# Selective scan: the B product, the carry copy and the C product of two state groups as one instruction of twice the width

## The chip, the core and the metric

The kernel runs on one core of a Trainium2 chip. The metric is the device time of one execution in microseconds (us); lower is better. The engines named below are TensorE (PE in the profile, its weight loads PEld), VectorE (DVE), ScalarE (ACT), GpSimd (POOL) and SyncE (SP), which issues every DMA of this kernel.

## What is computed

The input is a batch of eight images of 96 channels on 64 x 64 pixels, all in float32. Layer 0 is a state-space block: group norm, layer norm, an input projection, a depthwise 3x3 convolution with SiLU, a selective scan in four directions, an output norm with a gate, an output projection, and a small convolution branch. Layer 1 is a linear attention without softmax and a feed-forward network in a low-precision format. What fills the time is the scan of layer 0:

```python
def step(h, inp):
    u_t, d_t, b_t, c_t = inp
    dA = jnp.exp(d_t[..., None] * A)
    h = dA * h + (d_t * u_t)[..., None] * b_t[:, :, None, :]
    y = jnp.einsum('bkdn,bkn->bkd', h, c_t)
    return (h, y)
```

It runs over 4,096 steps, for 8 images, 4 directions, 192 channels and 16 states each.

## The kernel before

The images are taken in four pairs. For a pair `p`, a direction `k` (0 to 3) and a piece `ci` of 1,024 of the 4,096 steps there are three jobs, one for each tile `T` of 128 rows: channels 0 to 127 of the first image, the same of the second, and the remaining 64 channels of both. Within a job, a group `j` (0 to 3) is 32 of those 128 channels. A group is four units, `q` = 0 to 3: one unit holds 32 channels x 4 states on 128 partitions and 1,024 time steps along the free axis. There are 192 jobs, 768 groups and 3,072 units. The main loop goes over the units two at a time, which gives 1,536 passes, here called pairs of units.

One unit is worked like this:

- `spread` (once for each group, TensorE): matmuls with a selection matrix copy the group's rows of `du` (delta times u) four times onto 128 partitions of the PSUM tile `pu` of 1,024 columns. There is one such tile.
- `weights` (SyncE): DMAs bring the unit's rows of B and C, broadcast to the 32 channels, as the SBUF tiles `bm` and `cm`. They stay for several groups and are loaded again when the image or the piece changes.
- `decay` (ScalarE): `da` is exp(delta * A), one instruction for each unit, at most four units ahead.
- `scan` (VectorE): the B product `pb = pu * bm` into PSUM (two tiles, one for each unit of the pair), then the recurrence itself, `hc = scan(da, pb)`, from PSUM and SBUF into SBUF. In the first piece of a direction the scan begins at zero, in the other three at the stored `carry`.
- `scan` (GpSimd): where a further piece follows, the last column of `hc` is copied to `carry`; then the C product `hc = hc * cm` in place.
- `total` (once for each group, TensorE): matmuls with `add` sum the four states on neighbouring partitions and the four units into the PSUM tile `yp`. ScalarE copies that to `y` and SyncE stores it. It is recorded one group late.

The order of all instructions on TensorE, VectorE, ScalarE and GpSimd is the order in which the Python code records them (`InOrder`, whose line 266 is therefore the line of nearly all of them in the profile). For one pair it is: background work by `slots.run()`, `scan` for both units, the loads of B for two pairs ahead and of C for one pair ahead, the two `decay`s of the next pair, and at `q` = 2 also `spread` of the next group and `total` of the one before; then `slots.run()` again. `slots.run()` records a little of the other work of the block (norms, convolutions, projections, gates, the step sizes of the next job) on TensorE, ScalarE, GpSimd and SyncE, under a budget for each slot; VectorE has next to nothing else while the scans go on.

In `scan`, the order on VectorE for one pair is: product of the first unit, product of the second, scan of the first, scan of the second. On GpSimd it is: carry, C product, carry, C product. `bm` has four buffers, `cm` five, `hc` eight, `da` four, each of 1,024 columns. Four of PSUM's eight banks hold the two `pb` tiles, two hold `pu`, and `yp` and `pg` have one each. The framework adds the semaphore waits: an instruction that reads or overwrites what another one wrote or reads waits for a count of the other's engine, and it does so too where both are on the same engine.

Of the kernel before, what the change touches and what calls it, by code (L numbers as in the profile page):

```python
# [9 lines left out]
F32 = mybir.dt.float32  # L10
# [4 lines left out]
ALU = mybir.AluOpType  # L15
# [12 lines left out]
CH = 1024  # L28
NCH = L // CH
# [321 lines left out]
def phase_b(  # L351
# [7 lines left out]
    nc = tc.nc  # L359
    with ExitStack() as ctx:  # L360
# [57 lines left out]
        for i in range(2):  # L418

            t = cp.tile([C + 1, 512], F32, name=f"tn{i}")  # L420
            nc.gpsimd.memset(t[C : C + 1, :], 1.0)
            tns.append(t)
        inner = ExitStack()
        bcp = inner.enter_context(tc.tile_pool(name="b_bc", bufs=4))
        wp = inner.enter_context(tc.tile_pool(name="b_w", bufs=2))
        hp = inner.enter_context(tc.tile_pool(name="b_h", bufs=8))
        gp = inner.enter_context(tc.tile_pool(name="b_bg", bufs=1))
        psc = inner.enter_context(tc.tile_pool(name="b_ps", bufs=1, space=PSUM))

# [4 lines left out]
        yps = psc.tile([128, 512], F32, name="yp")  # L434
        bank0 = psc.tile([128, 512], F32, name="pg")
        pu = psc.tile([128, CH], F32, name="pu")
        pbs = [psc.tile([128, CH], F32, name=f"pb{i}") for i in range(2)]
        pe = InOrder(tc, nc.tensor, mybir.EngineType.PE)
        ve = InOrder(tc, nc.vector, mybir.EngineType.DVE)
        se = InOrder(tc, nc.scalar, mybir.EngineType.Activation)  # L440
        ge = InOrder(tc, nc.gpsimd, mybir.EngineType.Pool)
# [5 lines left out]
            for ci in range(NCH) for T in (0, 2, 1)  # L447
        ]
        units = [(job, j, q) for job in range(len(jobs)) for j in range(4) for q in range(4)]
        carries, bcs, dus, dls, sts, das, hcs, prevs, yet = ({} for _ in range(9))  # L450
        turned, resting, squeezed_at = set(), set(), set()

        def where(job):
            p, k, ci, T = jobs[job]
            c = NCH - 1 - ci if k >= 2 else ci
            return p, k, ci, c, T, slice(c * CH, c * CH + CH)

        def batch(u):
            job, j, q = units[u]
            T = jobs[job][3]  # L460
            return j // 2 if T == 2 else T
# [806 lines left out]
        def weights(u, i):  # L1268

            if u >= len(units):  # L1270
                return
            job, j, q = units[u]
            p, k, ci, c, T, at = where(job)
            b = batch(u)
            if (job // 3, b, q, i) in bcs:
                return
            t = bcp.tile([128, CH], F32, name=("bm", "cm")[i], bufs=(4, 5)[i])
            r0 = 32 * (k // 2) + 16 * i + 4 * q
            nc.sync.dma_start(
                t, xd_d[k % 2][2 * p + b][r0 : r0 + 4, at].unsqueeze(0).to_broadcast([32, 4, CH])  # L1280
            )
            bcs[job // 3, b, q, i] = t

# [27 lines left out]
        def scan(u):  # L1311

            job, j, q = units[u]
            p, k, ci, c, T, at = where(job)
            step, last = (-1, 0) if k >= 2 else (1, CH - 1)
            for i in range(2):
                ve.tensor_mul(pbs[i], pu, bcs[job // 3, batch(u), q + i, 0])
            for i in range(2):
                t = hp.tile([128, CH], F32, name="hc")
                carry = carries[p, k][:, T, 4 * j + q + i : 4 * j + q + i + 1]  # L1320
                ve.tensor_tensor_scan(
                    t[:, ::step], das.pop(u + i)[:, ::step], (pbs[i])[:, ::step],
                    0.0 if ci == 0 else carry, ALU.mult, ALU.add,
                )
                hcs[u + i] = t
            for i in range(2):
                v = u + i
                carry = carries[p, k][:, T, 4 * j + q + i : 4 * j + q + i + 1]
                if ci < NCH - 1:
                    ge.tensor_copy(carry, hcs[v][:, last : last + 1])  # L1330
                ge.tensor_mul(hcs[v], hcs[v], bcs[job // 3, batch(u), q + i, 1])

        def before(g):

# [14 lines left out]
        def total(g):  # L1349


            job, j, _ = units[4 * g]
            p, k, ci, c, T, at = where(job)
            yp = yps[:, 0:256]
            if k >= 2:
                pe.matmul(yp, ident, prevs.pop(g), start=True, stop=False)
            if k == 2 and p > 0:
                pe.matmul(yp, ident, yet.pop(g), start=False, stop=False)
            for n in range(4):
                for i in range(4):  # L1360
                    pe.matmul(
                        yp[32 * i : 32 * i + 32, :], add,
                        hcs[4 * g + n][:, 256 * i : 256 * i + 256],
                        start=(n == 0 and k < 2), stop=(n == 3),
                    )
            for n in range(4):
                hcs.pop(4 * g + n)
            y = wp.tile([128, 256], F32, name="y")
            to = y_d if k == 2 else ys_d[1]

            def store():
                if k < 2:
                    nc.sync.dma_start(ya_d[k % 2][p][T][c, j], y)
                    return
                for i in range(4):
                    nc.sync.dma_start(
                        to[p][T][
                            32 * j : 32 * j + 32, c * CH + 256 * i : c * CH + 256 * i + 256
                        ],
                        y[32 * i : 32 * i + 32, :],  # L1380
                    )

            slots.after(1, lambda: se.copy(y, yp))
            slots.after(4, store)
# [4 lines left out]
        n = len(units)  # L1389
# [3 lines left out]
        for u in range(4):  # L1393
            weights(u, 0)
        for u in range(2):
            weights(u, 1)
# [3 lines left out]
        for u in range(0, n, 2):  # L1400
            g, q = divmod(u, 4)
            if q == 0:
                if g % 4 == 0:
                    job = g // 4 + 1
                    assert slots.first is None
                    p, k, ci, T = jobs[g // 4]
# [15 lines left out]
                    if job < len(jobs):  # L1422
                        p, k, ci, c, T, at = where(job)
# [4 lines left out]
            elif g + 2 < n // 4:  # L1428
                fetch(g + 2)
            slots.run()  # L1430
            scan(u)
            for v in range(u + 4, u + 6):
                weights(v, 0)
# [4 lines left out]
            if q == 2:  # L1438
                if g + 1 < n // 4:
                    spread(g + 1)  # L1440
                if g > 0:
                    total(g - 1)
# [3 lines left out]
        slots.run()  # L1446
        slots.run()
        total(n // 4 - 1)
        while not slots.idle():
            slots.run()  # L1450
# [18 lines left out]
        p = NP - 1  # L1469
# [336 lines left out]
def block(tc, a, out):  # L1806
    with tc.tile_pool(name="dram", bufs=1, space=DRAM) as dp:
# [29 lines left out]
        with tc.tile_pool(name="p_const", bufs=1) as pp:  # L1837
            phase_b(
                tc, a, pp, xi_d, xd_d, dl_d, ya_d, ys_d, y_d, zs_d, inp_d, x1_d, ua_d, u_d, g_d,
                cb_d, tn_d, out,  # L1840
            )
# [105 lines left out]
```

## Time and profile before

| | us |
|---|---|
| median of 3 runs | 11066.46 |
| the runs | 11069.53, 11062.12, 11066.46 |
| span of the profiled execution, first to last instruction | 11058.4 |
| VectorE busy in it | 10525.7 (95%) |
| GpSimd busy in it | 9028.7 (82%) |
| TensorE busy in it | 7887.2 (71%) |
| ScalarE busy in it | 6596.3 (60%) |
| VectorE: 3,072 B products, 128x1024 | 3601.6 (mean of one 1.220) |
| VectorE: 2,304 scans with a carry | 5276.8 (mean 2.334) |
| VectorE: 768 scans from zero | 1713.1 (mean 2.275) |
| GpSimd: 3,072 C products, 128x1024 | 7230.0 (mean 2.359) |
| GpSimd: 2,304 carry copies, 128x1 | 422.5 (mean 0.183) |

Of the profiled execution no time beside its span is listed. The median lies 8.1 us above the span, which is taken as what lies around it. The busy time of a row is the union of its instructions, so where instructions of one row overlap it is less than count times mean. The B products run from 214.6 us to 10719 us; ahead of them lie the norms and convolutions of the first pair of images, behind them the tail for the last pair.

### The profile page before, as it was taken

What the parts mean: (1) busy time and instruction counts of PE and PEld (TensorE: products, weight loads), DVE (VectorE), ACT (ScalarE), POOL (GpSimd) and SP (SyncE); (2) the same over time, 40 slices, a digit from 0 to 9 for tenths busy, and PEclk for the clock granted to TensorE, in tenths of its full rate; (3) what the DMA queues carried; (4) which work ended last, traced back from release to release, by engine and by line L of the source; (5) the groups of instructions that cost most, each with busy time, mean ns of one, the idle gap of its engine ahead of it and who ended that gap; (6) DMA issues with size and microseconds to landing.
All of it is one profiled execution on the core that took longest, in us unless ns stands there. A gap on an engine that the chain in (4) does not pass through costs nothing.

```text
span 11058.4 us, 128094 instructions
## 1 busy us (share of the span) xinstructions
PE 7887.2 (71%) x39468; PEld 3111.6 (28%) x39468; DVE 10525.7 (95%) x6651; ACT 6596.3 (60%) x9175; POOL 9028.7 (82%) x6649
## 2 busy tenths in 40 slices
PE   7755778655568887767777787776767776665778
PEld 3322333222223332223222332223322222222223
DVE  4999999999999999999999999999999999999974
ACT  2544765544567666556776656565776656665554
POOL 2788877787898888998888887899889888988860
PEclk8877888877788888878878888887878877777889
DMA  3445554454555555666545555566544555644551
GB/s 117 151 165 180 160 156 157 141 188 156 163 185 172 171 172 157 211 214 195 158 152 160 157 178 159 177 220 209 172 157 159 160 164 179 197 157 140 173 157 37
DMA packets 900188, 1834.20 MB, mean 166 GB/s; under 512 B 247965, under 2 KB 421214, under 8 KB 892462
## 3 DMA queue, kind: packets, MB, share of 16 engines
q1 hardware_dynamic: 899502, 1826.01, 52.8%
q8 instruction: 314, 5.14, 0.2%
q14 instruction: 372, 3.05, 0.1%
HBM read 1405.13 MB, written 420.42 MB: 165 GB/s over the span
## 4 chain that ended last, share of the span: by engine, by line
PE 32%; issue 29%; DVE 17%; POOL 11%; ACT 6%; DMA 4%; SPq 0%; DVEq 0%; POOLq 0%; ACTq 0%
PE pu L266 12%; PE yp L266 11%; DVE hc L266 11%; POOL hc L266 7%; PE pg L266 6%; DVE pb L266 5%; ACT u L266 2%; ACT da L266 2%; POOL u L266 2%; PE t L266 2%; PE ps L197 1%; DMA bm<-xd 1%; POOL turn L266 1%; POOL carry L266 1%; ACT L266 1%
## 5 line engine op out<-in xcount | busy, mean ns | idle before, releaser
L266 POOL TENSOR_TENSOR hc<-hc,cm 128x1024 f32<-128x1024 f32 x3072 | 7230.0, 2359 | 591.0 <-DVE hc L266 382.6
L266 DVE TENSOR_TENSOR_SCAN hc<-da,carry,pb 128x1024 f32<-128x1024 f32 x2304 | 5276.8, 2334 | 38.1 <-ACT da L266 31.5
L266 PE MATMUL pu<-du,c_sel 128*128 128x512 f32 x3072 | 2452.5, 944 | 2244.1 <-DVE pb L266 2239.6
L266 DVE TENSOR_TENSOR pb<-pu,bm 128x1024 f32<-128x1024 f32 x3072 | 3601.6, 1220 | 133.9 <-PE pu L266 105.9
L266 ACT ACTIVATE da<-dl,c_alog 128x1024 f32<-128x1024 f32 x3072 | 3352.8, 1140 | 91.4 <-DVE hc L266 73.8
L266 PEld LDWEIGHTS pu<-du,c_sel 128*128 128x128 f32 x3072 | 790.0, 281 | 3521.1 <-DVE pb L266 2784.8
L266 DVE TENSOR_TENSOR_SCAN hc<-da,pb 128x1024 f32<-128x1024 f32 x768 | 1713.1, 2275 | 38.9 <-ACT da L266 22.8
L266 ACT COPY y<-yp 128x256 f32<-128x256 f32 x768 | 284.4, 370 | 2348.9 <-PE yp L266 2198.4
L266 PE MATMUL yp<-hc,c_add 128*32 128x256 f32 x24576 | 1660.8, 416 | 22.6 <-ACT s L266 6.6
L266 PEld LDWEIGHTS yp<-hc,c_add 128*32 128x32 f32 x24576 | 768.6, 120 | 1200.1 <-issue 628.4
L266 POOL COPY carry<-hc 128x1 f32<-128x1 f32 x2304 | 422.5, 183 | 766.1 <-DVE hc L266 744.9
L266 ACT ACT_TABLE_LOAD x566 | 726.2, 1283 | 38.2 <-DMA cb<-zs 16.9
L266 ACT COPY u<-pg 128x512 f32<-128x512 f32 (+6 forms) x397 | 218.3, 550 | 712.3 <-PE pg L266 641.2
L266 POOL TENSOR_TENSOR u<-u,u 96x512 f32<-96x512 f32 (+1 forms) x426 | 537.5, 1269 | 105.9 <-ACT u L266 101.8
L266 POOL TENSOR_TENSOR du<-du,dls 128x1024 f32<-128x1024 f32 x192 | 452.7, 2358 | 91.5 <-ACT dls L266 91.1
L266 ACT COPY u<-yp 96x512 f32<-96x512 f32 (+6 forms) x347 | 188.0, 542 | 465.5 <-PE yp L266 404.5
L266 PE MATMUL pg<-ain,wmain 96*128 96x512 f32 x792 | 354.1, 599 | 0.0
L266 PE MATMUL pg<-ain,wmix 96*128 96x512 f32 x792 | 353.0, 598 | 0.0
L266 PE MATMUL yp<-prev,ident 128*128 128x256 f32 x768 | 321.9, 512 | 39.0 <-ACT u L266 27.4
L266 PEld LDWEIGHTS yp<-prev,ident 128*128 128x128 f32 x768 | 214.5, 283 | 381.8 <-issue 264.3
L266 PE MATMUL pg<-st,dtw 12*128 12x512 f32 x384 | 218.5, 649 | 49.4 <-ACT u L266 28.8
L266 PE MATMUL yp<-st,dtw 12*128 12x512 f32 x384 | 227.9, 674 | 18.3 <-ACT u L266 10.9
(340 smaller groups left out, 7030.2 us busy)
## 6 DMA issues: line engine op xcount, KB each, us to landing
dl<-dl SPq DMA_DIRECT2D x768, 512.0 KB
bm<-xd SPq DMA_DIRECT2D x512, 512.0 KB
cm<-xd SPq DMA_DIRECT2D x512, 512.0 KB
du<-xi SPq DMA_DIRECT2D x192, 512.0 KB
dl<-dls SPq DMA_DIRECT2D x192, 512.0 KB
ya<-y SPq DMA_DIRECT2D x384, 128.0 KB
prev<-ya SPq DMA_DIRECT2D x384, 128.0 KB
xi<-u SPq DMA_DIRECT2D x152, 256.0 KB
```

The costliest lines, as they stand in the source:

```text
L197: nc.tensor.matmul(bank[r, :].rearrange("p (h w) -> p h w", w=W), w[:, t if len(which) > 1 or w is wmix else 0, columns], pads[b][:, 8 * j ...
L266: op(*args, **kw)
```

## The change

The two units of a pair share tiles of twice the width. `pb` becomes one PSUM tile of 2 x 1,024 columns in the same four banks, `hc` one SBUF tile of 2 x 1,024 with four buffers in place of eight, `bm` and `cm` tiles of 2 x 1,024 with two and three buffers, each still filled by two DMAs of the same size as before. The B product of a pair is then one VectorE instruction of 2,048 columns, in which `pu` is read twice by a step of zero. The carry copy is one GpSimd instruction of two columns, and the C product one GpSimd instruction of 2,048. The scans stay single. `total` reads the halves of the wide tiles with the same matmuls. The extra buffer space for `cm` (4 KB on each partition) comes from a smaller scratch area for DMAs that GpSimd would issue; here it issues none.

The order on VectorE for a pair becomes: product of both, scan of the first, scan of the second. On GpSimd: carry of both, C product of both.

```diff
-        hp = inner.enter_context(tc.tile_pool(name="b_h", bufs=8))
+        hp = inner.enter_context(tc.tile_pool(name="b_h", bufs=4))
...
-        pbs = [psc.tile([128, CH], F32, name=f"pb{i}") for i in range(2)]
+        pb = psc.tile([128, 2, CH], F32, name="pb")
...
-            t = bcp.tile([128, CH], F32, name=("bm", "cm")[i], bufs=(4, 5)[i])
+            if q % 2 == 0:
+                pairs[job // 3, b, q, i] = bcp.tile(
+                    [128, 2, CH], F32, name=("bm", "cm")[i], bufs=(2, 3)[i]
+                )
+            t = pairs[job // 3, b, q - q % 2, i]
             r0 = 32 * (k // 2) + 16 * i + 4 * q
             nc.sync.dma_start(
-                t, xd_d[k % 2][2 * p + b][r0 : r0 + 4, at].unsqueeze(0).to_broadcast([32, 4, CH])
+                t[:, q % 2, :], xd_d[k % 2][2 * p + b][r0 : r0 + 4, at].unsqueeze(0).to_broadcast([32, 4, CH])
             )
...
+            ve.tensor_mul(
+                pb, pu.unsqueeze(1).to_broadcast([128, 2, CH]), bcs[job // 3, batch(u), q, 0]
+            )
+            t = hcs[u] = hp.tile([128, 2, CH], F32, name="hc")
+            at = 4 * j + q
+            carry = carries[p, k][:, T, at : at + 2]
             for i in range(2):
-                ve.tensor_mul(pbs[i], pu, bcs[job // 3, batch(u), q + i, 0])
-            for i in range(2):
-                t = hp.tile([128, CH], F32, name="hc")
-                carry = carries[p, k][:, T, 4 * j + q + i : 4 * j + q + i + 1]
                 ve.tensor_tensor_scan(
-                    t[:, ::step], das.pop(u + i)[:, ::step], (pbs[i])[:, ::step],
-                    0.0 if ci == 0 else carry, ALU.mult, ALU.add,
+                    t[:, i, ::step], das.pop(u + i)[:, ::step], pb[:, i, ::step],
+                    0.0 if ci == 0 else carry[:, i : i + 1], ALU.mult, ALU.add,
                 )
-                hcs[u + i] = t
-            for i in range(2):
-                v = u + i
-                carry = carries[p, k][:, T, 4 * j + q + i : 4 * j + q + i + 1]
-                if ci < NCH - 1:
-                    ge.tensor_copy(carry, hcs[v][:, last : last + 1])
-                ge.tensor_mul(hcs[v], hcs[v], bcs[job // 3, batch(u), q + i, 1])
+            if ci < NCH - 1:
+                ge.tensor_copy(carry, t[:, :, last])
+            ge.tensor_mul(t, t, bcs[job // 3, batch(u), q, 1])
...
-                        hcs[4 * g + n][:, 256 * i : 256 * i + 256],
+                        hcs[4 * g + n - n % 2][:, n % 2, 256 * i : 256 * i + 256],
...
-    nc = bacc.Bacc("TRN2", target_bir_lowering=False, num_devices=1)
+    nc = bacc.Bacc(
+        "TRN2", target_bir_lowering=False, num_devices=1, dynamic_dma_scratch_size=1024
+    )
```

More of the change, by code (lines that the diff above doesn't have):

```diff
@@ L449, in phase_b @@
         units = [(job, j, q) for job in range(len(jobs)) for j in range(4) for q in range(4)]
-        carries, bcs, dus, dls, sts, das, hcs, prevs, yet = ({} for _ in range(9))
+        carries, bcs, pairs, dus, dls, sts, das, hcs, prevs, yet = ({} for _ in range(10))
         turned, resting, squeezed_at = set(), set(), set()
@@ L1362, in total @@
                         yp[32 * i : 32 * i + 32, :], add,
-                        hcs[4 * g + n][:, 256 * i : 256 * i + 256],
+                        hcs[4 * g + n - n % 2][:, n % 2, 256 * i : 256 * i + 256],
                         start=(n == 0 and k < 2), stop=(n == 3),
                     )
-            for n in range(4):
+            for n in range(0, 4, 2):
                 hcs.pop(4 * g + n)
```

## The prediction, written before the changed kernel ran

> **What bounds the kernel now.** I read the page's busy lines first, then the costliest groups, the idle time ahead of the B product's tile, and the VectorE timeline, in the loop and in the tail.
>
> ```profile
> PE 7887.2 (71%) x39468; PEld 3111.6 (28%) x39468; DVE 10525.7 (95%) x6651; ACT 6596.3 (60%) x9175; POOL 9028.7 (82%) x6649
> ...
> DVE 4999999999999999999999999999999999999974
> ...
> L266 POOL TENSOR_TENSOR hc<-hc,cm 128x1024 f32<-128x1024 f32 x3072 | 7230.0, 2359 | 591.0 <-DVE hc L266 382.6
> L266 DVE TENSOR_TENSOR_SCAN hc<-da,carry,pb 128x1024 f32<-128x1024 f32 x2304 | 5276.8, 2334 | 38.1 <-ACT da L266 31.5
> L266 DVE TENSOR_TENSOR pb<-pu,bm 128x1024 f32<-128x1024 f32 x3072 | 3601.6, 1220 | 133.9 <-PE pu L266 105.9
> ```
>
> VectorE is at nine tenths or more in 37 of 40 slices, and its work there is B products and scans alone. The idle time ahead of them is 211 us (38.1 + 38.9 + 133.9), 20 us of it at the very first product. GpSimd waits for VectorE's `hc`, not the reverse. So the end is set by the VectorE time of a pair, 1,536 times. The next view is the VectorE timeline (start, time, instruction, and idle time in brackets), first in the loop:
>
> ```profile
> 5001.25 2.34 DVE L266 TENSOR_TENSOR pb<-pu,bm 128x1024 f32<-128x1024 f32 x2
> 5003.50 4.57 DVE L266 TENSOR_TENSOR_SCAN hc<-da,carry,pb 128x1024 f32<-128x1024 f32 x2
> 5007.99 2.34 DVE L266 TENSOR_TENSOR pb<-pu,bm 128x1024 f32<-128x1024 f32 x2
> ```
>
> A pair takes 5007.99 - 5001.25 = 6.74 us, less than the durations (2 x 1.22 + 2 x 2.33 = 7.10): each instruction begins about 0.09 us before the one ahead ends (5001.25 + 2.34 - 5003.50). Taken from the trace's starts, the four steps have medians of 1.116 (product to product), 1.130 (to scan), 2.254 (scan to scan) and 2.238 (to the next product), 6.738 in all; from zero (one pair in four) they are 1.116 + 1.130 + 2.194 + 2.177 = 6.617.
>
> **Who may overlap.** VectorE instructions here wait for counts of VectorE itself. In the built program of before, a scan waits for its own product and a product for the scan that last read its `pb`, and in both cases one other instruction lies between. In the changed program the two waits that are left are for the instruction directly ahead:
>
> ```
> before: product 0   product 1   scan 0 (waits: product 0)   scan 1 (waits: product 1)
>         next product 0 (waits: scan 0)   next product 1 (waits: scan 1)
> after:  product     scan 0 (waits: product)   scan 1 (no VectorE wait)
>         next product (waits: scan 1)
> ```
>
> The trace of before has such adjacent pairs only in the tail, where the CAST waits for the TENSOR_SCALAR ahead of it, and `up` for the instruction ahead of it:
>
> ```profile
> L266 DVE CAST h<-w_dt.float 128x512 fp8e5<-128x512 f16 x48 | 21.3, 445 | 1.7
> ...
> 10954.78 0.34 DVE L266 TENSOR_SCALAR w_dt.float<-w_dt.float,b1f 128x512 f16<-128x512 f16 x1
> 10955.16 0.43 DVE L266 CAST h<-w_dt.float 128x512 fp8e5<-128x512 f16 x1
> ...
> 10807.15 0.73 DVE L266 SCALAR_TENSOR_TENSOR w_dt.float<-t,c_vec,w_dt.float 96x512 f32<-96x512 f32 x1
> 10807.99 0.48 DVE L266 TENSOR_SCALAR up<-w_dt.float,c_vec 96x512 f32<-96x512 f32 x1
> ```
>
> All 48 CASTs begin 0.035 us after the end (1.7 / 48), not 0.09 before it. The `up` begins 0.107 after (0.84 - 0.73): its VectorE wait stands in a separate wait instruction ahead of it, as it has a second wait, where the CAST has one. For a scan with its three or four waits (TensorE; VectorE with ScalarE; GpSimd) the nearest row is one that a late `da` releases through the same wait instruction:
>
> ```profile
> 423.87 1.15 ACT L266 ACTIVATE da<-dl,c_alog 128x1024 f32<-128x1024 f32 x1
> ...
> 425.11 2.35 DVE L266 TENSOR_TENSOR_SCAN hc<-da,carry,pb 128x1024 f32<-128x1024 f32 x1 [0.93 <-ACT da L266]
> ```
>
> It begins 0.09 after the end (425.11 - 425.02), and 0.09 is what the other such cases show too.
>
> **The change, part by part.**
>
> *Fewer products on VectorE.* 1,536 instructions of 1,024 columns go and the other 1,536 double. A product that does not overlap its predecessor takes 1.233 (those after an idle time). The second 1,024 columns add between 1.047 a thousandth each, i.e. 1.07 (from 0.684 for 512 columns, `tn<-t` in the tail, to 1.220 for 1,024: 0.536 / 512 each), and 1.116, the step from product to product. I take 1.07, as it is the rate and not an instruction's start: the wide product takes 2.30, bounds 2.30 and 2.35. A zero step on `pu` has no row; nothing in the trace has an access pattern that slows a row, and I take none.
>
> [...]
>
> *Two adjacent waits on VectorE.* Product to scan: 2.30 + 0.09 = 2.39, where the two products took 1.116 + 1.130 = 2.246: +0.143. Scan to scan: a scan that begins without overlap takes 2.347, against 2.340, and the second still overlaps it: +0.007. Scan to next product: the second scan's 2.324, then 0.035 where the product waits for VectorE alone (768 of 1,536) and 0.107 where it also waits for a new `pu`, 0.071 in the mean: 2.395 against 2.238, +0.157. The sum is +0.307 us a pair (+0.306 from zero), so 1,536 x 0.307 = +471 us, all on the engine that sets the end. With 0.035 at both places it would be +0.217, or +333; with 0.107 at both and 2.35 for the product, +0.41, or +630.
>
> *Relief of waits.* The longer pair gives the others time. The 43 waits for `da` (54 us, 1.3 each) lose about 0.4 each, and the 45 for `pu` (106 us) about 0.6 each, the length that a group gains in two pairs: 17 + 27 = 44. At some hundred stalled places the new wait hides in the old one: 100 x 0.15 = 15. Against it stand the loads of `bm`: their buffer comes free only at the end of the wide product, 1.1 later for the first half; 25 us of waits in 19 cases could grow by 10. I take -50, bounds 0 and -100.
>
> *GpSimd.* The wide C product has between 4.53 (2.359 + 1,024 x 2.125 ns, the slope from 1.271 at 512 columns) and 4.72; with one carry copy less (0.18 and its gap) a pair falls from 5.15 to about 4.8. The work waits beside VectorE's 6.7 and moves nothing while covered. But it can begin only after the second scan, 2.25 later than now. `total` reads the product one group later: in the timeline around 5000 us GpSimd ends a pair 3 to 5 us after its scans, `total` comes some 14 us after them. The delay of about 2.2 is covered; at the very end it is not: +2.
>
> *SyncE and TensorE.* The same DMAs, in the same sizes. With three wide buffers the first load of `cm` for a new image finds a free one, so SyncE waits there less; nothing queued behind it is late on VectorE now, so 0. A scan needs its `hc` buffer back from eight matmuls of `total` in place of four, about 0.5 us later; the waits of this kind (18.7 us, 6 cases) grow by at most 3. The smaller scratch costs 0, as every DMA in the queue table is issued by SyncE.
>
> **Sum.** 11058.4 + 471 - 50 + 5 = 11484 for the span, +8 around it: 11492, or 3.8% over the median. Bounds: +333 - 100 gives 11300, +630 gives 11700, whose ends need every term to fall on one side.
>
> **Rivals.**
>
> 1. *The overlap stays and the count decides* (faster). If the wait for the instruction ahead does not hold back the start, the pair loses 1.116 - 1.07 = 0.046 us: 1,536 x 0.046 = 71 us, so 10995. For it: the loop's own waits on VectorE counts cost nothing now. Against it: those are for the last instruction but one, and all 48 CASTs and the 15 `v` products that wait for the one ahead begin 0.035 late. It decides from the point where both adjacent boundaries still overlap by some 0.06, since an overlapped product of 2.28 with scans of 2.254 and 2.324 makes 6.858, 0.12 more than the pair now.
>
> 2. *Only short waits* (slower, but less): 0.035 at both places, +333 - 60: 11340. Against it: the scan's VectorE wait sits in the separate wait instruction, the form that showed 0.09.
>
> 3. *GpSimd becomes late* (slower, more). If its later start reaches `total`, TensorE holds back `pu` behind it, and each of 768 groups could pay part of 2.2 us: a quarter of them at 1 us gives +190 beside the rest, 11680. Against it: TensorE waited only 1.3 us in all for `hc` from GpSimd, whose load for a pair falls while the pair gets longer.
>
> **Chances and range.** The adjacent waits at about their forecast price 0.70; rival 2 0.14; rival 3 0.07; rival 1 0.08; no net difference (a cheaper wait that just eats the saving) 0.01. A change within 0.2% (22 us), about what a measurement of this kernel can tell from none, would need a gain and a loss to cancel. So faster 0.08, same 0.01, slower 0.91. The range holds rival 2 and most of the main case: 11310 to 11590.
>
> **What would show it.** In the profile after, the wide product should read 2.30 (right) with a gap ahead of it of 0.035 or 0.11 put down to VectorE's `hc`, and the first scan of a pair a gap of 0.09 put down to VectorE's `pb`; a pair from product to product 7.04, VectorE busy about 10750 (10525.7 and what no longer overlaps), and its idle time up by some 200 us. GpSimd falls to about 8550. A pair at 6.69 would make rival 1 right; many waits of TensorE for GpSimd's `hc`, rival 3.

## The result, and the profile after

The changed kernel takes 11501.81 us (median of 5 runs, 11498.14 to 11502.94) against 11069.53 before (5 runs, 11062.12 to 11075.09): 1.0391 times as long, 95% interval 1.0378 to 1.0403. It is slower by 432 us; forecast were 11492 and a range of 11310 to 11590. The profiled execution took 11502.25, with a span of 11500.2.

The page of the changed kernel, in the lines that answer to those of before:

```profile
PE 7965.5 (69%) x39468; PEld 3136.3 (27%) x39468; DVE 10736.3 (93%) x5115; ACT 6606.6 (57%) x9175; POOL 8630.2 (75%) x3961
...
DVE 4999999999999999999999999999999999999974
...
L266 POOL TENSOR_TENSOR hc<-hc,cm 128x2048 f32<-128x2048 f32 x1536 | 6960.4, 4531 | 737.8 <-DVE hc L266 518.3
L266 DVE TENSOR_TENSOR_SCAN hc<-da,carry,pb 128x1024 f32<-128x1024 f32 x2304 | 5281.4, 2334 | 168.9 <-ACT da L266 8.4
...
L266 DVE TENSOR_TENSOR pb<-pu,bm 128x2048 f32<-128x2048 f32 x1536 | 3532.2, 2300 | 188.2 <-PE pu L266 59.7
```

VectorE has 1,536 instructions fewer, and each wide product is cheaper than the two it replaces (2.300 us against 2 x 1.220). Yet VectorE is busy for 211 us more, since at two of the three places in a pair its instructions no longer overlap, and idle for longer: ahead of the scans with a carry 168.9 us against 38.1, of which waits for `da` explain 8.4. GpSimd is busy for 398 us less, and that bought nothing. The granted TensorE clock is 0.802 in place of 0.815, but that is not what costs: VectorE's waits for TensorE's `pu` fall from 106 to 60 us.

The VectorE timeline in the loop shows the gaps one by one (start, time, instruction):

```profile
5003.86 2.30 DVE L266 TENSOR_TENSOR pb<-pu,bm 128x2048 f32<-128x2048 f32 x1
5006.30 4.46 DVE L266 TENSOR_TENSOR_SCAN hc<-da,pb 128x1024 f32<-128x1024 f32 x2
5010.79 2.30 DVE L266 TENSOR_TENSOR pb<-pu,bm 128x2048 f32<-128x2048 f32 x1
```

The product ends at 5006.16 and the scan begins at 5006.30, where it began 0.09 ahead of the end before; the next product begins 0.03 after the second scan's end (5006.30 + 4.46). The two scans still overlap. These are scans from zero; with a carry, the medians of the trace's starts are 2.433 from product to scan, 2.264 to the second scan and 2.39 in the mean to the next product (2.321 and a gap of 0.07), 7.09 us a pair in place of 6.738.

### The profile page after: what moved, and what is told of

Its sections match the earlier page's. It is cut to its first block, busy times and chain, and to the rows that moved or that the text cites. A ratio compares the mean times of both kernels' runs of the same rounds, so it can differ in the third digit from the quotient of the medians.

```text
span 11500.2 us, 119630 instructions
## 1 busy us (share of the span) xinstructions
PE 7965.5 (69%) x39468; PEld 3136.3 (27%) x39468; DVE 10736.3 (93%) x5115; ACT 6606.6 (57%) x9175; POOL 8630.2 (75%) x3961
## 5 line engine op out<-in xcount | busy, mean ns | idle before, releaser
L266 POOL TENSOR_TENSOR hc<-hc,cm 128x2048 f32<-128x2048 f32 x1536 | 6960.4, 4531 | 737.8 <-DVE hc L266 518.3
L266 DVE TENSOR_TENSOR_SCAN hc<-da,carry,pb 128x1024 f32<-128x1024 f32 x2304 | 5281.4, 2334 | 168.9 <-ACT da L266 8.4
L266 PE MATMUL pu<-du,c_sel 128*128 128x512 f32 x3072 | 2523.2, 969 | 2696.4 <-DVE pb L266 2691.8
L266 DVE TENSOR_TENSOR pb<-pu,bm 128x2048 f32<-128x2048 f32 x1536 | 3532.2, 2300 | 188.2 <-PE pu L266 59.7
L266 POOL COPY carry<-hc 128x2 f32<-128x2 f32 x1152 | 215.7, 187 | 1617.3 <-DVE hc L266 1552.7
```

The source lines that it names most:

```text
L266: op(*args, **kw)
```

## The experiments

Two theories were open. A: two VectorE instructions now wait for the one directly ahead of them, because both units share a tile. B: the loss comes from the wide work itself, be it VectorE's wide product or GpSimd's wide and later C product.

**The product split again.**

```diff
-        pb = psc.tile([128, 2, CH], F32, name="pb")
+        pbs = [psc.tile([128, CH], F32, name=f"pb{i}") for i in range(2)]
...
-            ve.tensor_mul(
-                pb, pu.unsqueeze(1).to_broadcast([128, 2, CH]), bcs[job // 3, batch(u), q, 0]
-            )
+            for i in range(2):
+                ve.tensor_mul(pbs[i], pu, bcs[job // 3, batch(u), q, 0][:, i, :])
...
-                    t[:, i, ::step], das.pop(u + i)[:, ::step], pb[:, i, ::step],
+                    t[:, i, ::step], das.pop(u + i)[:, ::step], (pbs[i])[:, ::step],
```

> The changed kernel, with the B product split again into two instructions of 1,024 columns that write two separate PSUM tiles; the wide bm, cm and hc, the wide carry copy, the wide C product and the small DMA scratch stay. If the adjacent VectorE waits are the cause, the pair falls from 7.09 us back to 6.74 and the time to that of before, 11067 us, less at most 20 for what the lighter GpSimd frees: 11045 to 11075. If GpSimd's later and wider work or the wide buffers are the cause, it stays near 11500.

Measured: 11060.96 us against 11066.02, ratio 0.9997 (0.9988 to 1.0006): no difference that can be told from none. Its VectorE timeline is that of before again, 6.74 us a pair:

```profile
5000.86 2.33 DVE L266 TENSOR_TENSOR pb<-pu,bm 128x1024 f32<-128x1024 f32 x2
5003.11 4.57 DVE L266 TENSOR_TENSOR_SCAN hc<-da,carry,pb 128x1024 f32<-128x1024 f32 x2
5007.60 2.33 DVE L266 TENSOR_TENSOR pb<-pu,bm 128x1024 f32<-128x1024 f32 x2
```

So the wide `hc`, `bm` and `cm`, GpSimd's wide instructions, the bulk of the change by lines, and the smaller scratch cost and gain nothing together. What costs is in the one edit undone here, the wide product with its shared tile.

**GpSimd's work split again**, the wide product kept:

```diff
-            if ci < NCH - 1:
-                ge.tensor_copy(carry, t[:, :, last])
-            ge.tensor_mul(t, t, bcs[job // 3, batch(u), q, 1])
+            for i in range(2):
+                if ci < NCH - 1:
+                    ge.tensor_copy(carry[:, i : i + 1], t[:, i, last : last + 1])
+                ge.tensor_mul(t[:, i, :], t[:, i, :], bcs[job // 3, batch(u), q, 1][:, i, :])
```

> The changed kernel, with the carry copy and the C product split again into two instructions each, on the halves of the wide hc; the wide B product stays. If the adjacent VectorE waits are the cause, nothing on VectorE changes: 11500 us, 11490 to 11520, the same gaps of 0.133 us ahead of the first scan of a pair and 0.035 or 0.10 ahead of the product. If the wide GpSimd work is the cause, it falls to about 11070.

Measured: 11504.02 us, 1.0397 (1.0382 to 1.0411), the time of the changed kernel. All of the loss is on VectorE's side. That leaves the width of the product against the waits.

**Adjacent waits without any width.** In the kernel before, the product of each unit is put directly ahead of its scan:

```diff
             for i in range(2):
                 ve.tensor_mul(pbs[i], pu, bcs[job // 3, batch(u), q + i, 0])
-            for i in range(2):
                 t = hp.tile([128, CH], F32, name="hc")
```

> The kernel before, with nothing but the order on VectorE changed: product of the first unit, its scan, product of the second unit, its scan. No instruction is wide. Each scan now waits for the instruction directly ahead of it, and no product has a wait on VectorE left. If adjacent waits are the cause, each of the two scans begins 0.133 us after its product ends in place of 0.094 before, and the scan that starts late takes 0.01 longer: a pair of 2 x (1.21 + 0.133 + 2.26) = 7.20 us against 6.74, 1,536 x 0.46 = 710 us less some 120 of relief, so about 11650. If the width of the product or of GpSimd's work is the cause, there is nothing of it here and the time stays at 11067.

Measured: 12812.16 us, 1.1578 (1.1563 to 1.1594), far over the 11650 expected. The VectorE timeline:

```profile
5000.46 1.21 DVE L266 TENSOR_TENSOR pb<-pu,bm 128x1024 f32<-128x1024 f32 x1
5001.80 2.35 DVE L266 TENSOR_TENSOR_SCAN hc<-da,carry,pb 128x1024 f32<-128x1024 f32 x1
5004.06 1.21 DVE L266 TENSOR_TENSOR pb<-pu,bm 128x1024 f32<-128x1024 f32 x1
...
5012.74 1.23 DVE L266 TENSOR_TENSOR pb<-pu,bm 128x1024 f32<-128x1024 f32 x1 [1.39 <-PE pu L266]
```

The steps are as expected: 1.342 from product to scan (gap 0.133) and 2.263 from scan to product, 7.21 us a pair, which makes 1,536 x 0.47 = 725 us. The other 1,020 us are waits like that in the last line; they stand in the view of VectorE's waits (total us, times, longest):

```profile
DVE pb L266 <- PE pu L266: 870.0, 642, 20.3
DVE hc L266 <- PE yp L266: 258.6, 272, 5.0
```

In the kernel before they were 105.9 in 45 cases and 18.7 in 6. The edit moved product 1 behind scan 0, and product 1 is what frees `pu`: TensorE then has one scan (2.26 us) to refill it in place of two (4.49). That this is why TensorE came late is read from the order, not tested alone. The expectation had not counted who else waits for a step that is moved. Theory A stands, but this run is no clean measure of it.

**The same two adjacent waits, with `pu` freed as before.** Only the products change places (both entries of each tuple are the same here, so `odd` decides nothing; the scans keep their order):

```diff
-            for i in range(2):
+            odd = u // 2 % 2
+            scans = ((0, 1), (0, 1))[odd]
+            for i in ((1, 0), (1, 0))[odd]:
                 ve.tensor_mul(pbs[i], pu, bcs[job // 3, batch(u), q + i, 0])
```

> The kernel before with single tiles and single instructions; only the two products of a pair change places on VectorE: product 1, product 0, scan 0, scan 1. So scan 0 waits for the product directly ahead of it, and the next product 1 for the scan directly ahead of it, as in the changed kernel, while pu comes free no later than before. If adjacent waits are the whole cause, the pair is 1.14 (a product that starts late, then overlaps) + 1.34 (1.21 + 0.133) + 2.264 + 2.39 = 7.14 us, 0.40 over before and 0.05 over the changed kernel, which alone has the saving of width: about 11580, 11550 to 11610. If width is the cause, 11067.

Measured: 11587.14 us, 1.0473 (1.0458 to 1.0489). Its timeline:

```profile
5004.24 2.36 DVE L266 TENSOR_TENSOR pb<-pu,bm 128x1024 f32<-128x1024 f32 x2
5006.74 4.59 DVE L266 TENSOR_TENSOR_SCAN hc<-da,carry,pb 128x1024 f32<-128x1024 f32 x2
5011.36 1.23 DVE L266 TENSOR_TENSOR pb<-pu,bm 128x1024 f32<-128x1024 f32 x1
```

This pair is 7.12 us long, with 0.14 ahead of the scan and 0.03 ahead of the next product. Two instructions of the old kernel in the other order cost more than the whole change (524 us against 432). The changed kernel is 85 us faster than this one (11587 - 11502), about 0.055 us a pair. Since `split_product` showed the rest of the change to be worth nothing, that is what the width of the product gains.

**The two waits one by one.** The order of the units alternates from pair to pair, so that only one kind of adjacent wait is left in each kernel (decays, carry copies and C products follow the scans). The diff is that of raw_only; in war_only the products, too, go `((0, 1), (1, 0))`:

```diff
-            for i in range(2):
+            odd = u // 2 % 2
+            scans = ((0, 1), (1, 0))[odd]
+            for i in ((1, 0), (0, 1))[odd]:
                 ve.tensor_mul(pbs[i], pu, bcs[job // 3, batch(u), q + i, 0])
-            for i in range(2):
+            for i in scans:
                 t = hp.tile([128, CH], F32, name="hc")
```

> The kernel before, with the two units of a pair in another order by turns: product 1, product 0, scan 0, scan 1, and in the next pair product 0, product 1, scan 1, scan 0 (decays, carry copies and C products follow the order of the scans). Only the first scan of a pair waits for the instruction directly ahead; a product overwrites what the last scan but one read. If the two adjacent waits add up, this one alone costs 1.342 - 1.130 + 0.010 = 0.22 us a pair, 341 us less some 60 of relief: about 11340, 11300 to 11390. If only the two together matter, or width, 11067.

> The kernel before, with the other half: product 0, product 1, scan 0, scan 1, and in the next pair product 1, product 0, scan 1, scan 0. Only the first product of a pair waits for the scan directly ahead, whose input it overwrites; each scan reads what the last product but one wrote. If the waits add up, 2.39 - 2.238 + 0.023 = 0.176 us a pair, 270 us less some 50 of relief: about 11285, 11250 to 11330. Rival, that a wait to overwrite costs VectorE nothing where a wait to read does: 11067.

Measured: 11360.99 us, 1.0270 (1.0253 to 1.0287), for the wait of a scan to read its product, and 11293.85 us, 1.0208 (1.0192 to 1.0223), for the wait of a product to overwrite a scan's input. The VectorE timelines of raw_only and of war_only (the brackets hold ordinary waits for others):

```profile
5003.86 2.36 DVE L266 TENSOR_TENSOR pb<-pu,bm 128x1024 f32<-128x1024 f32 x2 [4.41 <-PE pu L266]
5006.35 4.47 DVE L266 TENSOR_TENSOR_SCAN hc<-da,pb 128x1024 f32<-128x1024 f32 x2
5010.73 2.34 DVE L266 TENSOR_TENSOR pb<-pu,bm 128x1024 f32<-128x1024 f32 x2
```

```profile
5002.61 4.46 DVE L266 TENSOR_TENSOR_SCAN hc<-da,pb 128x1024 f32<-128x1024 f32 x2 [1.23 <-POOL hc L266]
5007.11 2.36 DVE L266 TENSOR_TENSOR pb<-pu,bm 128x1024 f32<-128x1024 f32 x2
5009.38 4.45 DVE L266 TENSOR_TENSOR_SCAN hc<-da,pb 128x1024 f32<-128x1024 f32 x2
```

In the first the gap of 0.13 stands ahead of the scan alone and the next product overlaps; in the second a gap of 0.04 stands ahead of the product alone and the scan overlaps. Over the 11063.43 of before they are 298 and 230 us, 528 together; the kernel with both is 524 over it. The two waits add up, and a wait to overwrite is not free.

**One tile, two single products.**

```diff
-            ve.tensor_mul(
-                pb, pu.unsqueeze(1).to_broadcast([128, 2, CH]), bcs[job // 3, batch(u), q, 0]
-            )
+            for i in range(2):
+                ve.tensor_mul(pb[:, i, :], pu, bcs[job // 3, batch(u), q, 0][:, i, :])
```

> The changed kernel with its wide pb tile, but two products of 1,024 columns, one into each half. The waits are set for the tile and not for its halves: the second product waits for the first, the first scan for the second product, and the next product for the last scan, three adjacent waits in a pair. If these are the cause, the pair is 1.268 + 1.366 + 2.264 + 2.39 = 7.29 us: 11067 + 846 - 110, about 11800, slower than the changed kernel. If the width of the instruction is the cause, it goes back to 11067, as with two separate tiles (11061).

Measured: 11774.33 us, 1.0642 (1.0626 to 1.0658). Its VectorE timeline:

```profile
5000.36 4.58 DVE L266 TENSOR_TENSOR_SCAN hc<-da,carry,pb 128x1024 f32<-128x1024 f32 x2
5004.98 2.50 DVE L266 TENSOR_TENSOR pb<-pu,bm 128x1024 f32<-128x1024 f32 x2
5007.61 4.59 DVE L266 TENSOR_TENSOR_SCAN hc<-da,carry,pb 128x1024 f32<-128x1024 f32 x2
```

The kernel with the same single products and two tiles took 11061 us; this one takes 713 us more. Its two products no longer overlap either (2.50 us for both, against 2.33), although they write different halves: the framework sets its waits for the tile and not for its halves. With that, theory B is out: no wide VectorE instruction is in this kernel, and it is slower than the change.

**The wide product without an adjacent wait.** This needs a second wide `pb`. Every other pair has it in SBUF, and the product of the next pair is put between the two scans of this one (`spread` of the next group is recorded ahead of the scans, to be in time for it):

```diff
+        pbs = [
+            psc.tile([128, 2, CH], F32, name="pb0"), gp.tile([128, 2, CH], F32, name="pb1")
+        ]
...
                     0.0 if ci == 0 else carry[:, i : i + 1], ALU.mult, ALU.add,
                 )
+                if i == 0 and u + 2 < len(units):
+                    product(u + 2)
```

> The changed kernel with two wide pb tiles by turns, one in PSUM and one in SBUF (there is no more room in PSUM), and the product of the next pair between the two scans of this one. The wide product stays; every VectorE wait is again for the last instruction but one. If adjacent waits are the cause, all gaps ahead of products and scans close and the pair costs 6.738 - 1.116 + 1.07 = 6.69 us: 11067 - 71 = 10995, provided that a scan reading pb from SBUF costs what one from PSUM costs. If the wide product is slow in itself, the pair stays near 7.1 and the time near 11500. Open in both: whether VectorE reading two SBUF operands slows GpSimd's C product, 4.53 us now.

Measured: 13086.44 us, 1.1825 (1.1809 to 1.1841), far over the 10995 expected. The waits behaved: the gaps are gone, and the step over the wide product is 2.182 us. What failed is the condition of the expectation, that a scan from SBUF costs what one from PSUM costs: such scans last too long. VectorE and GpSimd in the same stretch:

```profile
5002.65 2.27 DVE L266 TENSOR_TENSOR pb<-pu,bm 128x2048 f32<-128x2048 f32 x1
5004.83 6.91 DVE L266 TENSOR_TENSOR_SCAN hc<-da,pb 128x1024 f32<-128x1024 f32 x2
5011.67 2.26 DVE L266 TENSOR_TENSOR pb<-pu,bm 128x2048 f32<-128x2048 f32 x1
```

```profile
5000.52 2.19 POOL L266 COPY carry<-hc 128x2 f32<-128x2 f32 x1
5002.79 4.63 POOL L266 TENSOR_TENSOR hc<-hc,cm 128x2048 f32<-128x2048 f32 x1
5009.63 0.19 POOL L266 COPY carry<-hc 128x2 f32<-128x2 f32 x1 [2.21 <-DVE hc L266]
```

The first of the two scans reads `pb` from SBUF. It is recorded from 5004.83 to 5009.57, 4.74 us, and ends 2.15 after GpSimd's C product (5002.79 + 4.63 = 5007.42). Of the 1,536 scans from SBUF (mean 3.58 us; the others have 2.31) 1,004 began while a GpSimd instruction had 0.2 us or more still to run, and the middle nine tenths of these end 2.145 to 2.153 us after that one's end. The other way round, a carry copy of 0.19 took 2.19 while such a scan ran; the 502 copies that began during one have a median of 2.16, the 504 that began during a scan from PSUM one of 0.187. So in this run the two did not go on at the same time.

**The same with GpSimd mostly idle**, by leaving out the C product (`ge.tensor_mul(t, t, ...)`):

> The kernel of product_between without GpSimd's C product: the scanned states go to the sum over states unweighted, so this part of the computation is left out. GpSimd keeps the carry copies and the background work, some 1.5 ms in all. If VectorE scans that read pb from SBUF last long only because they and GpSimd's instructions exclude each other, then with GpSimd mostly idle they fall from 3.58 us to near 2.3, and the order with the wide product in between shows its own price: a pair of 6.68 us, 11067 less some 75, plus up to 250 for the collisions that are left: 10990 to 11250. If reading pb from SBUF makes the scan slow in itself, it stays near 13000.

and its control, the kernel before without its C product:

> The kernel before without GpSimd's C product (that part of the computation is left out), as the control of between_no_c. On VectorE nothing changes but the waits for others: the pair stays at 6.74 us, and of the 190 us of waits in the loop up to 80 may go, as in between_no_c. So 10985 to 11065. If it comes to 10994 like between_no_c or below, the order with the wide product in between gains nothing that could be measured there; if it stays at 11060, the 73 us there are the order's.

Measured: 10993.98 us, 0.9934 (0.9917 to 0.9950) of before, and for the control 10950.72, 0.9898 (0.9881 to 0.9916). The groups of VectorE in between_no_c (count, busy us, mean ns, idle us before):

```profile
L266 DVE TENSOR_TENSOR_SCAN hc<-da,carry,pb 128x1024 f32<-128x1024 f32 x2304 | 5343.5, 2357 | 7.3 <-ACT da L266 4.4 <-PE yp L266 2.5
L266 DVE TENSOR_TENSOR pb<-pu,bm 128x2048 f32<-128x2048 f32 x1536 | 3481.0, 2266 | 101.7 <-PE pu L266 77.5 <-DMA bm<-xd 23.8
```

The scans with a carry are back at 2.357 us, near the 2.334 of before (2.957 in product_between). Those from SBUF alone fall to 2.38 in the mean (2.334 in the median of the 644 that met no GpSimd instruction, against 2.330 from PSUM), so they are not slow in themselves, and the step medians make 2.182 + 2.241 + 2.256 = 6.68 us a pair, 0.06 under before, as computed. But that is 91 us, and the scans that still meet GpSimd's background work give it back: (2.38 - 2.31) x 1,536 = 108 us. VectorE's waits of over 0.15 us in the loop are 27 us longer too (110 against 83 in the control). Against its control this order is 43 us slower (10993.98 - 10950.72). Without the control its 75 us (11068.66 - 10993.98) would have looked like a gain of the order; they come from GpSimd's missing work. So what a wide product gains where every wait is covered is known here from the step medians alone. No version was found that beats the kernel before.

## Why the prediction was right

**What bounds the kernel.** Right: VectorE is at nine tenths or more in 37 of 40 slices after as before, what its pair of units costs more appears in the total, and 398 us less of GpSimd bought nothing.

**The adjacent waits.** Right, and shown by undoing and redoing each alone. Of the terms:

| | forecast, us | measured, us |
|---|---|---|
| wide product | 2.30 | 2.300 |
| gap from product to scan | 0.09 | 0.133 |
| scan to scan, more than before | 0.007 | 0.010 |
| gap ahead of the product (times) | 0.035 / 0.107 | 0.035 (754) / 0.09 to 0.105 (726) |
| pair, more than before | 0.307 | 0.35 |
| for 1,536 pairs | +471 | +535 |
| relief of waits for others | -50 | about -95 |
| time around the span | +8 | 2 |

The relief is what 535 leaves of the 442 by which the span grew (11500.2 - 11058.4).

The gap of the scan was mis-sized by 0.043. Its row of before was a scan released by a late `da`, through a wait instruction that holds two counts, VectorE's and ScalarE's. There the VectorE count had long been reached. In the changed kernel it is the VectorE count that comes last; the trace shows the product's end at 5006.163, the wait instruction from 5006.202 to 5006.251, and the scan at 5006.295. In the kernel before, a wait instruction of VectorE with two counts takes these 0.05 also where it holds nothing up (5002.498 to 5002.548; 0.047 to 0.052 in 2,826 of 3,208), and one with a single count 0.021 (all 4,126), as ahead of `up`. In the row of before the wait instruction stood from 423.089, was held by ScalarE's count alone, and ended at 425.066, 0.045 after ScalarE's end (425.021) and 0.045 ahead of the scan (425.111): 0.09 in all. So the nearest row had the right instruction but the wrong count in it.

The relief was too small by about 45. Waits of over 0.15 us ahead of VectorE's loop instructions (without the very first) fell from 189 us in 117 cases to 116 in 82; those for `da` from 54 to 24 and for `pu` from 106 to 60, where 17 and 27 had been allowed. Presumably a slack that grows with every pair is not spent at one wait but keeps later ones from building up; no run shows that by itself, and some 20 us of the relief lie in no wait that was counted. The 8 us around the span came from setting a median beside the span of one short execution; where both are of one execution they lie 2 us apart (11502.25 and 11500.2). The two large errors, +64 and -45, nearly cancel: that the total came within 10 us is luck, and better than its terms.

**GpSimd, SyncE, TensorE.** Right: the wide C product takes 4.531 (forecast 4.53), TensorE waits 4.1 us in all for GpSimd's `hc` (1.3 before), waits for `bm` are 23 us, as before (25). GpSimd's busy time fell to 8630, not to about 8550, which costs nothing here.

**The rivals.** The saving of the wide product exists (85 us by `swap_products`, where rival 1 had 71) but is outweighed. Short waits only: the product's are short in half the cases, the scan's all but never (3 of 1,536 are under 0.12). A late GpSimd: not there (the 4.1 us above).

## What to carry to other kernels

Before two instructions are made one, look at what stood between a producer and its consumer: with two units in flight each instruction began about 0.09 us before the one ahead ended, and one instruction for both put a dependence next to its source at both of its ends. Where VectorE sets the end, count for each instruction how many others lie between it and the one it waits for; none costs 0.12 to 0.23 us here (a gap of 0.035 to 0.133 in place of an overlap of 0.09), against 0.05 that the width saves. A shared tile also shares its waits (`one_tile` is 713 us over `split_product`, with the same two products in two tiles), and a control with the same work left out belongs to every run that leaves work out.

## What the runs showed of the hardware

- On VectorE, a product or scan of the changed kernel that waits for the instruction directly ahead began 0.035 us after its end, or 0.09 to 0.133 where the wait stands in a separate wait instruction; without such a wait the next began 0.08 to 0.09 before the end (medians 0.083 there, 0.085 to 0.094 in the kernel before). A wait to overwrite delayed as a wait to read did (230 us in `war_only`, 298 in `raw_only`).
- In `product_between`, a VectorE scan with both tensors in SBUF and the GpSimd copies and products did not run at the same time (4.74 us for a scan of 2.3, 2.19 for a copy of 0.19). With `pb` in PSUM they did: a copy kept its 0.187 us beside such a scan.
- GpSimd's C product, off the path, still costs 113 us (11063.59 - 10950.72): without it, the waits of over 0.15 us in VectorE's loop fall from 189 to 83 us, those for `bm` from 25 to 1 and for `pu` from 106 to 52. Yet `split_product`, with 404 us less on GpSimd, is no faster. Through which queue the C product delays the others was not taken apart and stays open.
